# A hybrid transformer block on one core: the mixer's TensorE order written out, and work moved between its blocks

## The chip, the cores and the metric

The kernel runs on one core of a Trainium2 chip. A core has five engines with a queue of instructions each: TensorE (PE in the profile; its weight loads are shown apart as PEld) multiplies matrices, VectorE (DVE) and ScalarE (ACT) work on elements, GpSimd (POOL) works on elements in SBUF too, and SyncE (SP) issues the transfers (DMA) between the chip's memory and the core's SBUF. TensorE writes its results to PSUM, from where VectorE or ScalarE take them. Each queue is worked through in its order; an instruction that has to wait for another engine holds up all that stand behind it in the same queue.

The metric is the device time of one execution in microseconds (us). The median of three executions of the kernel before is 1883.2 us (1882.77 to 1884.28).

## The reference

Input x has 4 sequences of 256 tokens with 512 channels, in float32. Four residual parts follow each other, each behind a layer norm: attention, a feed-forward with a row and column selection, the mixer, and the same feed-forward again. All that matters here happens in the mixer, a state-space layer with 128 heads of 64 channels in 8 groups:

```
proj = input_states @ in_proj_w.T            # gate 8192, x 8192, B 8*128, C 8*128, dt 128
xBC  = silu(causal_conv4(proj[x, B, C]) + conv_b)
dA   = softplus(dt + dt_bias) * -exp(A_log)
y    = state space recurrence(x, B, C, dA, dt) + D * x      # group g: 16 heads share B[g], C[g]
g    = y * silu(gate)
g    = group rms norm(g) * norm_w                            # over each group's 1024 channels
out  = g @ out_w.T
```

The recurrence is a masked product over earlier tokens: for a head, y[i] is the sum over j <= i of (C[i] . B[j]) * exp(cum[i] - cum[j]) * dt[j] * x[j], with cum the running sum of dA. The output is x plus the mixer's out, through the last feed-forward.

## The kernel before

The mixer (`mixer`, from line 784) keeps the normed input in SBUF, split into a high and a low part (`mx0`, `mx1`), since every large product is made as three products of high and low parts (`mm3`, lines 113 to 115; so a row L113, L114 or L115 may belong to any of them). The tiles tell which: `pp` is a projection, `pog` an out product.

The 8192 channels are worked through in 64 blocks of 128 channels (two heads); eight blocks make a group. For block i:

- `projected("x", i)`: 24 matmuls of 512 columns into `pp`, a PSUM tile of two banks with two buffers. `conv` (lines 959 to 974) reads it: one ScalarE pass, three VectorE taps (L969), one ScalarE SiLU (L973).
- `product` (L1043): the weighted values of block i - 1, 32 matmul instructions from factors `em` and the turned values `xd` into `pyy`. `gated` (lines 1050 to 1067) adds D * x, multiplies by the gate, writes the result to memory (`spill`) and adds its square to the group's sum `sq` on GpSimd.
- `projected("g", i)`: 24 matmuls, then SiLU to `gt` on ScalarE.
- `differences` (lines 996 to 1014): the factors exp(cum[i] - cum[j]) of the two heads, from a row `r` of cumulated sums that a DMA spreads over the partitions (`rows`); VectorE, GpSimd and 18 ScalarE instructions. `weighted` (L1017) multiplies them by the group's masked scores `gm`.
- `turned` (lines 1019 to 1035): eight transposes of x into two one-bank tiles `trx` of the pool `m_m` (tag "m", two buffers), each evacuated by VectorE to `xd` with dt as a factor.

A group's scores (`scores`, lines 976 to 989) come from B and C, which are projected and convolved like x; `pg` lies in the same "m" buffers. A group's out product cannot start before its norm is known, so it runs one group late: in blocks 1 to 7 of the next group, `recall` reads eight spilled tiles of gated values back (`gr`), splits them into `gh`, and `partial` makes 24 matmuls into `pog`, also in "m"; `scaled` (L1114) adds the result to x. The weights of the out product come per block: `out_weights` (lines 1072 to 1082) loads 256 KB into `wor` (two buffers), scales on ScalarE (L1078) and takes the low part on VectorE (L1079) into `wo` (eight buffers, one per block of a group).

The input weights stream through `wr` (three buffers); `prepare` splits each piece of 128 columns two projections ahead, the high part on ScalarE (L105), the low part on GpSimd for the first five pieces and on VectorE afterwards (L106).

What sets the order: the source records the operations in the loop of lines 1150 to 1202, and a planner then orders each engine's queue by its own estimate of the times. So TensorE's order in the mixer is the planner's. It puts, for example, six matmuls of the next block's x ahead of block i's transposes, and sets an out product between the two halves of the transposes. In the attention part the order of TensorE is written by hand already (`tc.manual_schedule`). Each engine's queue, SP's too, is fixed when the program is built.

Of the kernel before, what the change touches and what calls it, by code (L numbers as in the profile page):

```python
# [9 lines left out]
F32 = mybir.dt.float32  # L10
# [21 lines left out]
NCL = 64  # L32
FH = (NCL + C) // 2
EPS = 1e-5


COLS = {}
# [40 lines left out]
def hybrid_kernel(  # L78
# [705 lines left out]
    def mixer(feed, later):  # L784
        with ExitStack() as es, ExitStack() as inner:
# [189 lines left out]

            def scores(bt, ct):

                gm = p2.tile([P, B, 3, P], F32, name="gm", tag="gm")
                for b in range(B):
                    pg = ps.tile([P, 3, P], F32, name="pg", tag="m")  # L980
                    k0, k1 = bt[:, b * L : b * L + P], bt[:, b * L + P : (b + 1) * L]
                    q1 = ct[:, b * L + P : (b + 1) * L]
                    nc.tensor.matmul(
                        pg[:, 0:2, :].rearrange("p s i -> p (s i)"), k0, ct[:, b * L : (b + 1) * L],
                        start=True, stop=True,
                    )
                    nc.tensor.matmul(pg[:, 2, :], k1, q1, start=True, stop=True)
                    nc.vector.tensor_tensor(gm[:, b], pg, tri.rearrange("p (s i) -> p s i", s=3), ALU.mult)
                return gm

            def rows(h):
                r = p2.tile([P, NT], F32, name="r", tag="r", bufs=2)
# [26 lines left out]
            def turned(n, x2):  # L1019

                xd = p2.tile([P, TT, P], F32, name="xd", tag="xd", bufs=1)
                for half in range(2):
                    yield xd
                    hs = slice(half * 4, half * 4 + 4)
                    tr = ps.tile([P, 4, P], F32, name="trx", tag="m")
                    for q in range(4):
                        c = half * 4 + q
                        nc.tensor.transpose(tr[:, q, :], x2[:, c * P : (c + 1) * P], ident)  # L1028
# [6 lines left out]
                yield  # L1035

            def product(xd, es2):
                py = ps_y.tile([P, B, L], F32, name="pyy", tag="pyy")
# [80 lines left out]
            order = [("b", 0), ("c", 0)]  # L1119
            for n in range(NB):  # L1120
                order += [("x", n), ("g", n)]
                if n % GB == 6 and n // GB + 1 < G:
                    order.append(("b", n // GB + 1))
                if n % GB == 7 and n // GB + 1 < G:
                    order.append(("c", n // GB + 1))
            at = {v: i for i, v in enumerate(order)}

            def projected(kind, n):
# [12 lines left out]
                return pp  # L1141

            bt = conv(projected("b", 0), NB, "gb", 3)
            ct = conv(projected("c", 0), NB + G, "gb", 3)
            gms = {0: scores(bt, ct)}
# [4 lines left out]
            for i in range(NB + 1):  # L1150
                g, gi = divmod(i, GB)
                if i < NB:
                    x2 = conv(projected("x", i), i, "x2", 2)
                if 1 <= i <= NB:
                    m = i - 1
                    px2, gt, xd, em = stage.pop(m)
                    py = product(xd, em)
                    sq = sqs.get(m // GB)
                    sqs[m // GB] = gated(m, px2, gt, py, sq)
                if i < NB:  # L1160
                    pp = projected("g", i)
# [8 lines left out]
                if gi == 0 and i >= GB:  # L1170
                    todo = [(g - 1, t) for t in range(TT)]
                if gi == 1 and i >= GB:
                    rgs[g - 1] = root(sqs.pop(g - 1))
                if i < NB:
                    turning = turned(i, x2)
                    xd = next(turning)
                    next(turning)
                for _ in range(PER.get(gi, 0)):
                    if recalled:
                        q, t, hl = recalled.pop(0)  # L1180
                        po = ps.tile([P, C], F32, name="pog", tag="m")
                        for half in range(2):
                            partial(po, q, hl[half], half)
                        scaled(q, t, po)
                if i < NB:
                    for _ in turning:
                        pass
                    if gi == 6 and g + 1 < G:
                        bt = conv(projected("b", g + 1), NB + g + 1, "gb", 3)
                    if gi == 7 and g + 1 < G:  # L1190
                        ct = conv(projected("c", g + 1), NB + G + g + 1, "gb", 3)
                        gms[g + 1] = scores(bt, ct)
                    for e in em:
                        weighted(e, gms[g])
                    stage[i] = (x2, gt, xd, em)
                for _ in range(PER.get(gi + 1, 0) if i < NB else 0):
                    if todo:
                        q, t = todo.pop(0)
                        recalled.append((q, t, [recall(q, t, half) for half in range(2)]))
                if gi >= 6 and g < G:  # L1200
                    ks = {6: (0, 1, 2, 3), 7: (4, 5, 6, 7)}[gi]
                    wos.setdefault(g, []).extend(out_weights(g, k) for k in ks)

            es_p.close()
            ps_o = pool("m_o", 4, space=PSUM, **freed)
# [52 lines left out]
def arrange(inputs):  # L1258
# [12 lines left out]
    for n in range(NB):  # L1271
        order += [NB + n, n]
        g, gi = divmod(n, GB)
        if g + 1 < G and gi == 6:
            order.append(2 * NB + g + 1)
        if g + 1 < G and gi == 7:
            order.append(2 * NB + G + g + 1)
# [49 lines left out]
```

## Time and profile before

| what | us |
|---|---|
| median of three executions | 1883.2 |
| the profiled execution | 1881.0 |
| its span, first to last instruction | 1879.2 |
| TensorE busy in the span | 1812.6 |
| VectorE busy | 1464.7 |
| ScalarE busy | 1367.7 |
| GpSimd busy | 397.0 |

The mean TensorE clock granted in the span is 0.989 of the full one. The mixer's blocks run from about 410 to 1795 us. The last feed-forward ends the program.

How to read the lines that follow. A line of a group or of the timeline names source line, engine, operation, output tile <- input tiles and shape. In the timeline the first two numbers are the start and the length in us, and a bracket gives how long the engine was idle before and what ended that. In the list of waits the three numbers are us in total, how often, and the longest. An engine's instructions overlap a little, so a stream's pace is read from start to start. Two facts about this kernel's lines: a matmul's end is modelled, and weighted values and scores show twice as many matmul instructions as the source has calls.

Over the mixer the starts of successive products (`pyy`) give the time of a block. One group, blocks 32 to 40:

| from product to product | us |
|---|---|
| blocks 32 to 33 | 28.4 |
| 33 to 37, each | 20.3 |
| 37 to 38, 38 to 39, 39 to 40 | 25.7, 27.0, 18.3 |
| eight blocks | 180.6 |

### The profile page before, as it was taken

The page shows a single profiled execution, that of the slowest core. Times are in us where ns is not written, and L with a number is a line of the kernel's source. Part 1 is how long each engine was busy: PE and PEld are TensorE (multiplying, and loading weights), DVE is VectorE, ACT ScalarE, POOL GpSimd, SP SyncE. Part 2 cuts the span into 40 slices and gives each one's busy share as a digit, 9 for nine tenths or more (in the row PEclk, how much of TensorE's full clock was granted, in tenths as well). Part 3 has the DMA queues.
Part 4 walks back from the last instruction along what each step waited for, and adds up shares of the span by engine and source line. Part 5 has one row for each costly group of instructions (what it writes and reads, how often), then busy time and mean ns, then how long its engine had stood idle before and what let it go on. Part 6 is the DMA issues. An engine that isn't in the chain of part 4 may idle for free.

```text
span 1879.2 us, 29896 instructions
## 1 busy us (share of the span) xinstructions
PE 1812.6 (96%) x10706; PEld 1450.4 (77%) x10706; DVE 1464.7 (78%) x2317; ACT 1367.7 (73%) x2809; POOL 397.0 (21%) x380
## 2 busy tenths in 40 slices
PE   7999988899999999999999999999999999999997
PEld 6777767677778787887787787878887888787787
DVE  5566667789997779778977787778778877877777
ACT  6666675378897778777876786778777876877754
POOL 6332230012321111221221121112221211121200
PEclk9999999899999999999999999999999999999999
DMA  4000000135555545544545455544444545455341
GB/s 144 1 1 1 22 15 13 37 99 170 185 182 166 156 148 173 152 157 146 185 140 172 144 173 155 165 147 162 157 157 140 179 145 164 152 159 161 113 125 50
DMA packets 152772, 240.35 MB, mean 128 GB/s; under 512 B 12464, under 2 KB 77616, under 8 KB 152624
## 3 DMA queue, kind: packets, MB, share of 16 engines
q1 hardware_dynamic: 152624, 238.44, 39.8%
q8 instruction: 84, 1.38, 0.3%
q14 instruction: 64, 0.52, 0.1%
HBM read 202.75 MB, written 35.65 MB: 127 GB/s over the span
## 4 chain that ended last, share of the span: by engine, by line
PE 79%; DVE 9%; ACT 7%; issue 2%; DMA 2%; POOL 1%; SPq 0%; DVEq 0%; ACTq 0%; POOLq 0%
PE pp L113 12%; PE pp L114 12%; PE pp L115 12%; PE pyy L1043 9%; PE pog L113 6%; PE pog L115 6%; PE pog L114 6%; PE trx L1028 3%; ACT e L475 2%; DVE acc L969 2%; PE ptr L491 1%; DMA wor<-in_wout_dram 1%; PE pq L113 1%; PE pq L114 1%; PE pq L115 1%
## 5 line engine op out<-in xcount | busy, mean ns | idle before, releaser
L113 PE MATMUL pp<-mx,w 128*128 128x512 f32 (+1 forms) x1160 | 465.2, 401 | 7.9 <-DVE acc L969 7.4
L114 PE MATMUL pp<-mx,w 128*128 128x512 f32 (+1 forms) x1160 | 454.0, 391 | 0.0
L115 PE MATMUL pp<-mx,w 128*128 128x512 f32 (+1 forms) x1160 | 453.7, 391 | 0.0
L969 DVE SCALAR_TENSOR_TENSOR acc<-pp,cw_s,acc 128x1012 f32<-128x1012 f32 (+2 forms) x240 | 305.3, 1272 | 23.0 <-ACT acc L962 22.3
L1017 DVE TENSOR_TENSOR em<-em,gm 128x1536 f32<-128x1536 f32 x128 | 228.6, 1786 | 94.3 <-ACT em L1011 85.9
L113 PEld LDWEIGHTS pp<-mx,w 128*128 128x128 f32 x1160 | 218.4, 188 | 65.7 <-issue 10.2
L1005 POOL TENSOR_SCALAR_AFFINE_SELECT r<-r 128x512 f32<-128x512 f32 x128 | 148.6, 1161 | 521.9 <-DMA r<-cumd 394.8
L1066 POOL TENSOR_TENSOR sq<-sq,acc 128x1024 f32<-128x1024 f32 x55 | 132.6, 2410 | 582.1 <-ACT acc L1065 582.1
L115 PEld LDWEIGHTS pp<-mx,w 128*128 128x128 f32 x1160 | 218.4, 188 | 45.5 <-issue 0.4
L114 PEld LDWEIGHTS pp<-mx,w 128*128 128x128 f32 x1160 | 218.6, 188 | 40.6 <-issue 0.7
L105 ACT CAST w<-wr 128x512 fp32r<-128x512 f32 x144 | 88.5, 615 | 188.9 <-PE pp L114 150.2
L113 PE MATMUL pog<-wo,gh 128*128 128x512 f32 x512 | 204.7, 400 | 0.0
L115 PE MATMUL pog<-wo,gh 128*128 128x512 f32 x512 | 200.0, 391 | 0.0
L1010 ACT ACTIVATE em<-r,col_t 128x128 f32<-128x128 f32 x512 | 165.0, 391 | 48.1 <-PE pyy L1043 46.5
L114 PE MATMUL pog<-wo,gh 128*128 128x512 f32 x512 | 200.0, 391 | 0.0
L1043 PE MATMUL pyy<-em,xd 128*64 128x256 f32 (+1 forms) x2048 | 189.1, 329 | 2.4 <-DVE em L1017 2.4
L1043 PEld LDWEIGHTS pyy<-em,xd 128*64 128x64 f32 x2048 | 133.9, 137 | 63.8 <-issue 21.8
L1013 ACT ACTIVATE em<-r,col_t 128x128 f32<-128x128 f32 x512 | 166.5, 388 | 0.0
L1001 DVE TENSOR_SCALAR em<-r,col_t 128x128 f32<-128x128 f32 x512 | 137.9, 332 | 12.1 <-PE pyy L1043 10.1
L1029 DVE TENSOR_TENSOR xd<-trx,dt_t 128x512 f32<-128x512 f32 x128 | 86.3, 684 | 54.1 <-PE trx L1028 53.9
L106 DVE TENSOR_TENSOR w<-wr,w 128x512 fp32r<-128x512 f32 x139 | 97.6, 703 | 35.9 <-ACT w L105 35.4
L475 ACT ACTIVATE e<-sc,nmx 128x256 f32<-128x256 f32 (+1 forms) x256 | 104.0, 441 | 21.0 <-DVE nmx L469 20.9
(290 smaller groups left out, 3187.2 us busy)
## 6 DMA issues: line engine op xcount, KB each, us to landing
wr<-in_win_dram SPq DMA_DIRECT2D x287, 256.0 KB, 2.8
r<-cumd SPq DMA_DIRECT2D x128, 512.0 KB, 4.1
spill<-gb SPq DMA_DIRECT2D x63, 512.0 KB, 2.8
gr<-spill SPq DMA_DIRECT2D x120, 256.0 KB, 3.5
wor<-in_wout_dram SPq DMA_DIRECT2D x64, 256.0 KB, 3.1
out_dram<-x SPq DMA_DIRECT2D x8, 256.0 KB, 2.3
x<-in_x_dram SPq DMA_DIRECT2D x1, 1536.0 KB, 8.7
gr<-spill SPq DMA_DIRECT2D x8, 192.0 KB, 2.5
```

The lines of the kernel that those rows point to most:

```text
L113: nc.tensor.matmul(o, lh, rh, start=(first and k == 0), stop=False)
L114: nc.tensor.matmul(o, lh, rl, start=False, stop=False)
L115: nc.tensor.matmul(o, ll, rh, start=False, stop=(last and k == n - 1))
L475: nc.scalar.activation(es_[c][:, 2 * j + pr, :], sc[:, j, :], AF.Exp, bias=nm[:, j : j + 1], accum_out=rs[:, c, h : h + 1],)
L969: nc.vector.scalar_tensor_tensor(av[:, :, d:], pv[:, :, : L - d], cw_s[:, ch, tap : tap + 1], av[:, :, d:], ALU.mult, ALU.add,)
L1001: nc.vector.tensor_scalar(e[:, b, 2, :], rv[:, b, 1, :], col_t[:, h, b, 1:2], 0.0, ALU.subtract, ALU.min,)
L1005: nc.gpsimd.affine_select(rv[:, :, 0, :], rv[:, :, 0, :], pattern=[[0, B], [1, P]], compare_op=ALU.is_ge, fill=-1e30, base=0, channel_mult ...
L1010: nc.scalar.activation(e[:, b, 1, :], rv[:, b, 1, :], AF.Exp, bias=col_t[:, h, b, 2:3])
L1013: nc.scalar.activation(e[:, b, 0, :], rv[:, b, 0, :], AF.Exp, bias=col_t[:, h, b, 0:1])
L1017: nc.vector.tensor_tensor(e, e, gm, ALU.mult)
L1043: nc.tensor.matmul(py[d, b, k * P :], xd[:, 2 * b + k, d], es2[hh][:, b, 2 * k : 2 if k == 0 else 3, :].rearrange("p s i -> p (s i)"), sta ...
L1066: (nc.gpsimd if n < NB - 1 else nc.vector).tensor_tensor(sq, sq, x2, ALU.add)
```

## The change

TensorE's order in the mixer's loop is written by hand, and the loop is rearranged:

1. B and C of the next group are projected behind blocks 5 and 6 of a group instead of 6 and 7 (`NEXT`; the order of the weight blocks in memory follows).
2. Within a block, the out product of the group before comes right behind x's projection; then the weighted values of block i - 1; then the second out product where there are two; then g's projection. In block 0 of a group, where there is no out product, the weighted values come between the halves of g's projection (`between`).
3. All eight transposes stand together, behind g's projection; both "m" buffers are taken at once.
4. The scores of a group are made in its block 0: two batches before g's projection, two after it. Before, they were made at the end of block 7. `gm` has one buffer instead of two, `em` four instead of three.
5. The out weights of pieces 0 to 3 of a group are asked for in its block 7, pieces 4 to 7 in block 0 of the next group. Before, this was blocks 6 and 7.
6. The low part of the input weights is taken on GpSimd for the first 18 pieces instead of 5.
7. The last block's weighted values, and pieces 4 to 7 of the last group's out weights, stand behind the loop.

```diff
+NEXT = {5: "b", 6: "c"}
...
-                    split(pieces[i], raws.pop(i), nc.gpsimd if i < 5 else nc.vector)
+                    split(pieces[i], raws.pop(i), nc.gpsimd if i < 18 else nc.vector)
...
-                gm = p2.tile([P, B, 3, P], F32, name="gm", tag="gm")
+                gm = p2.tile([P, B, 3, P], F32, name="gm", tag="gm", bufs=1)
+                yield gm
...
-                e = p2.tile([P, B, 3, P], F32, name="em", tag="em", bufs=3)
+                e = p2.tile([P, B, 3, P], F32, name="em", tag="em", bufs=4)
...
+                trs = [ps.tile([P, 4, P], F32, name="trx", tag="m") for _ in range(2)]
+                for c in range(TT):
+                    nc.tensor.transpose(trs[c // 4][:, c % 4, :], x2[:, c * P : (c + 1) * P], ident)
+                for half, tr in enumerate(trs):
...
+            with tc.manual_schedule(engines={nc.tensor.engine}):
+                for i in range(NB):
+                    g, gi = divmod(i, GB)
                     x2 = conv(projected("x", i), i, "x2", 2)
+                    if gi == 1 and g:
+                        rgs[g - 1] = root(sqs.pop(g - 1))
+                    outers = len(recalled)
+                    if outers:
+                        outer()
+                        inner_products(i - 1)
+                    while recalled:
+                        outer()
...
+                    if gi == 0 and g:
+                        scoring = scores(group["b"], group["c"])
+                        gm = next(scoring)
+                        next(scoring)
+                        next(scoring)
+                        todo = [(g - 1, t) for t in range(TT)]
+                    pp = projected("g", i, between)
...
+                    for _ in scoring:
                         pass
+                    xd = turned(i, x2)
+                    if gi in NEXT and g + 1 < G:
+                        convolved(NEXT[gi], g + 1)
                     for e in em:
+                        weighted(e, gm)
                     stage[i] = (x2, gt, xd, em)
+                    for _ in range(PER.get(gi + 1, 0)):
+                        if todo:
+                            q, t = todo.pop(0)
+                            recalled.append((q, t, [recall(q, t, half) for half in range(2)]))
+                    ks = {7: (0, 1, 2, 3), 0: (4, 5, 6, 7)}.get(gi, ())
+                    for k in ks:
+                        q = g if gi else g - 1
+                        if q >= 0:
+                            wos.setdefault(q, []).append(out_weights(q, k))
+            inner_products(NB - 1)
+            wos[G - 1].extend(out_weights(G - 1, k) for k in range(4, 8))
```

`outer()` is one tile's out product with its scaling; `inner_products(m)` is `product` and `gated` of block m; `convolved` is the projection and convolution of B or C.

More of the change, by code (lines that the diff above doesn't have):

```diff
@@ L988, in scores @@
                     nc.vector.tensor_tensor(gm[:, b], pg, tri.rearrange("p (s i) -> p s i", s=3), ALU.mult)
-                return gm
+                    yield
             def rows(h):
@@ L1021, in turned @@
                 xd = p2.tile([P, TT, P], F32, name="xd", tag="xd", bufs=1)
-                for half in range(2):
-                    yield xd
+                trs = [ps.tile([P, 4, P], F32, name="trx", tag="m") for _ in range(2)]
+                for c in range(TT):
+                    nc.tensor.transpose(trs[c // 4][:, c % 4, :], x2[:, c * P : (c + 1) * P], ident)
+                for half, tr in enumerate(trs):
                     hs = slice(half * 4, half * 4 + 4)
[L1025 to L1028, printed above, removed]
                     nc.vector.tensor_tensor(
@@ L1034, in turned @@
                     )
-                yield
+                return xd
             def product(xd, es2):
@@ L1121, in mixer, with projected @@
                 order += [("x", n), ("g", n)]
[L1122 to L1125, printed above, removed]
+                if n % GB in NEXT and n // GB + 1 < G:
+                    order.append((NEXT[n % GB], n // GB + 1))
             at = {v: i for i, v in enumerate(order)}
-            def projected(kind, n):
+            def projected(kind, n, between=lambda: None):
                 i = at[kind, n]
@@ L1140, in projected, with convolved, outer, inner_products @@
                     project(w, pp, slice(half * 512, half * 512 + 512))
-                return pp
-            bt = conv(projected("b", 0), NB, "gb", 3)
-            ct = conv(projected("c", 0), NB + G, "gb", 3)
-            gms = {0: scores(bt, ct)}
+                    if half == 0:
+                        between()
+                return pp
+            group = {}
+            def convolved(kind, g):
+                at_ = NB if kind == "b" else NB + G
+                group[kind] = conv(projected(kind, g), at_ + g, "gb", 3)
+            def outer():
+                q, t, hl = recalled.pop(0)
+                po = ps.tile([P, C], F32, name="pog", tag="m")
+                for half in range(2):
+                    partial(po, q, hl[half], half)
+                scaled(q, t, po)
+            def inner_products(m):
+                px2, gt, xd, em = stage.pop(m)
+                py = product(xd, em)
+                sqs[m // GB] = gated(m, px2, gt, py, sqs.get(m // GB))
+            convolved("b", 0)
+            convolved("c", 0)
+            scoring = scores(group["b"], group["c"])
+            gm = next(scoring)
+            for _ in scoring:
+                pass
             rr = {h: rows(h) for h in range(2)}
@@ L1149, in mixer, with between @@
             PER = {1: 2, 2: 1, 3: 1, 4: 1, 5: 1, 6: 1, 7: 1}
-            for i in range(NB + 1):
-                g, gi = divmod(i, GB)
-                if i < NB:
+            with tc.manual_schedule(engines={nc.tensor.engine}):
+                for i in range(NB):
+                    g, gi = divmod(i, GB)
                     x2 = conv(projected("x", i), i, "x2", 2)
[L1154 to L1161, printed above, removed]
+                    if gi == 1 and g:
[6 more added lines that the diff above has]
+                        outer()
+                    def between():
+                        if i and not outers:
+                            inner_products(i - 1)
+                    if gi == 0 and g:
+                        scoring = scores(group["b"], group["c"])
+                        gm = next(scoring)
+                        next(scoring)
+                        next(scoring)
+                        todo = [(g - 1, t) for t in range(TT)]
+                    pp = projected("g", i, between)
                     gt = p2.tile([P, NT], F32, name="gt", tag="gt", bufs=1)
@@ L1169, in mixer @@
                             rr[h + 2] = rows(h + 2)
[L1170 to L1184, printed above, removed]
@@ L1185, in mixer @@
-                if i < NB:
-                    for _ in turning:
-                        pass
[L1188 to L1192, printed above, removed]
+                    for _ in scoring:
+                        pass
+                    xd = turned(i, x2)
@@ L1193, in mixer @@
+                    if gi in NEXT and g + 1 < G:
+                        convolved(NEXT[gi], g + 1)
                     for e in em:
-                        weighted(e, gms[g])
+                        weighted(e, gm)
                     stage[i] = (x2, gt, xd, em)
[L1196 to L1199, printed above, removed]
@@ L1200, in mixer @@
-                if gi >= 6 and g < G:
-                    ks = {6: (0, 1, 2, 3), 7: (4, 5, 6, 7)}[gi]
-                    wos.setdefault(g, []).extend(out_weights(g, k) for k in ks)
+                    for _ in range(PER.get(gi + 1, 0)):
[7 more added lines that the diff above has]
+                            wos.setdefault(q, []).append(out_weights(q, k))
@@ L1273, in arrange @@
         g, gi = divmod(n, GB)
[L1274 to L1277, printed above, removed]
+        if g + 1 < G and gi in NEXT:
+            order.append(2 * NB + (0 if NEXT[gi] == "b" else G) + g + 1)
     blocks = wi[: (2 * NB + 2 * G) * P].reshape(-1, P, KC, P)[order]
```

## The prediction

> **What bounds the kernel now.** I read the page's shares and slices first, then the TensorE waits, then the timeline of one change of group. In the first view the reader is to see that TensorE alone is near full, and that from slice 9 on (the mixer, 410 to 1795 us) it shows nine tenths or more at a granted clock of one.
>
> ```profile
> PE 1812.6 (96%) x10706; PEld 1450.4 (77%) x10706; DVE 1464.7 (78%) x2317; ACT 1367.7 (73%) x2809; POOL 397.0 (21%) x380
> ...
> PE   7999988899999999999999999999999999999997
> ...
> PEclk9999999899999999999999999999999999999999
> ```
>
> Busy time hides small holes, so I go by starts. In the timeline matmuls of 512 columns start 0.227 us apart:
>
> ```profile
> 1246.59 0.47 PE L113 MATMUL pp<-mx,w 128*128 128x512 f32 x1 [0.88 <-DVE acc L969]
> 1246.90 0.39 PE L114 MATMUL pp<-mx,w 128*128 128x512 f32 x1
> 1247.13 0.40 PE L115 MATMUL pp<-mx,w 128*128 128x512 f32 x1
> 1247.36 0.40 PE L113 MATMUL pp<-mx,w 128*128 128x512 f32 x1
> ```
>
> A block of the steady part has 72 of them (24 for x, 24 for g, 24 for one out product): 16.3 us. Its product of weighted values takes 2.75, its eight transposes 0.79, and each change between kinds about 0.1. That makes 20.2; products start 20.3 us apart in blocks 2 to 5 of a group (1130.3, 1150.6, 1170.9). So there TensorE has no hole worth having. All that can be gained lies at the change of group: from product to product eight blocks later 180.6 us pass (1101.9 to 1282.5), while the work is 6 x 20.2 + 2 x 5.45 (B, C) + 17.4 (first block: no out product, eight score matmuls) + 27.5 (second block: two out products, group sum) = 177.1. Hence 3.5 us per change, seven changes, 24 us: the whole prize. The waits name its larger part:
>
> ```profile
> PE pp L113 <- DVE acc L969: 7.4, 8, 1.1
> ...
> PE pg L983 <- ACT acc L973: 2.8, 4, 0.9
> ```
>
> What now costs nothing, and why: a group's eight out-weight pieces pass through two "wor" buffers. A piece is a DMA, a ScalarE scaling, a VectorE remainder, and the next DMA starts when that remainder ends:
>
> ```profile
> 1259.87 0.37 SPq L1075 DMA_DIRECT2D wor<-in_wout_dram  x1
> 1262.86 0.33 SPq L1075 DMA_DIRECT2D wor<-in_wout_dram  x1
> 1265.31 0.33 SPq L1075 DMA_DIRECT2D wor<-in_wout_dram  x1
> ```
>
> ```profile
> 1262.08 0.75 DVE L1079 SCALAR_TENSOR_TENSOR wo<-wor,nw_s,wo 128x512 fp32r<-128x512 f32 x1 [0.41 <-ACT wo L1078]
> ...
> 1263.77 0.72 ACT L1078 ACTIVATE wo<-wor,nw_s 128x512 fp32r<-128x512 f32 x1 [1.72 <-DMA wor<-in_wout_dram]
> ...
> 1264.53 0.75 DVE L1079 SCALAR_TENSOR_TENSOR wo<-wor,nw_s,wo 128x512 fp32r<-128x512 f32 x1 [0.51 <-ACT wo L1078]
> ...
> 1272.84 0.74 DVE L1079 SCALAR_TENSOR_TENSOR wo<-wor,nw_s,wo 128x512 fp32r<-128x512 f32 x1
> ```
>
> The reader sees one buffer turn: DMA at 1259.87, ScalarE at 1263.77, VectorE to 1265.28, next DMA at 1265.31: 5.4 us. The last piece is done at 1273.6; the first out product that uses them ends at 1303.2, so some 24 us of cover.
>
> **The change, part by part.**
>
> *B and C behind blocks 5 and 6, scores split 2 + 2 around g.* Same 48 projection matmuls, same 16 score instructions. An out product and a weighted product now stand between a conv and the next use of its PSUM buffer, 13.8 us, against conv's 1.2 + 3 x 1.19 and its queue: the L969 wait goes. C's conv is a block early: the L983 wait goes.
>
> *Out products first.* The weighted product gets 5.45 us more time; its factors are weighted a block ahead, before g. Gain: the 2.4 us of such waits, mostly in group 0. Price: an out product follows x, so its recalled halves and weights are wanted 5.45 us into the block instead of after g, product and transposes, 9.5 us earlier. For the halves the reads have a block of 20.2 us: nothing. For the weights see below.
>
> *Transposes in eights.* 0.79 + 0.12 instead of 2 x (0.35 + 0.12): 0.03 us a block, 2 us in all. They need both "m" banks, so they wait for the evacuation of what lay there.
>
> *Splits on GpSimd up to piece 17.* 13 more remainders move from VectorE (0.60 us start to start) to GpSimd (1.63 us in its L106 row): 7.8 us off VectorE in group 0; there are two blocks of slack for each, beside 2.4 us sums and 0.8 us selects.
>
> *Four factor buffers, one mask buffer.* The mask's last reader is block 7's weighting, a block before. Nothing.
>
> *TensorE in written order.* Before, x's matmuls filled the waits. In the first block after the scores the chain of transposes, masks and x's SiLU is now bare: some 14 of 24 x matmuls that ran beside it move behind it, +3 us once. In group 0 ScalarE changes table four times a block instead of 2.8: 4 x 1.29 + 10.8 of work = 15.9 against 15.5 per block: +2 us. In the steady part that sum with the recalls is 17.0 under 20.2: covered. At the end the last product has no out product between its transposes, and the last group's weights come later: +3.
>
> *Out weights 4 to 7 moved from block 7 to the next group's block 0.* This decides. In the built program's order, with t from the start of block 0's x: TensorE x 5.45, scores 6.7, half g 9.4, product 12.35, half g 15.1, scores 16.3. VectorE can't touch the gated value before 12.35; then stand in its queue gb 1.19, its gate 1.13, seven differences at 0.25 (0.21 in a row, 0.33 alone) and among the last of them masks 2 and 3 at 0.47: 17.3. The transposes wait for both: TensorE loses 0.6, and x of block 1 ends at 23.25, the group sum at 24.95, the first half of the first out product at 27.7. Behind the masks VectorE has two xd 0.6, two weightings 1.67, a w remainder and a gh remainder 0.6: 23.2. SP's queue is in order: a weight load that waits for that w remainder, then a recall that waits for that gh remainder, and only behind them the DMAs of pieces 4 and 5, at 23.7 and 24.1. With 3.1 us to landing: 26.8 and 27.2. ScalarE's next entry there is the fourth recalled half (buffer free at 27.4), then piece 4: VectorE done 29.45; piece 5 behind a table load and an exp: 31.95. Pieces 6 and 7 take the buffers of 4 and 5 one turn (5.4 us) later: 35.1 and 37.4. TensorE waits in place, in four gaps, and ends the second half at 38.1 instead of 30.4: 7.7. Queued behind it are the weighted product, the second out product and g of block 1, so nothing covers it. Bounds: if the DMAs of 4 and 5 were not held up on SP, pieces 6 and 7 are ready some 4 us earlier (stall 4); with landing at that row's longest, 5.3 instead of 3.1, twice in the chain, 12. I take 7.7, which the turn of the trace gives.
>
> [...]
>
> [...]
>
> **Sum.** Against the profiled execution, 1881.0 us for a span of 1879.2: per change 177.1 + 0.6 + 7.7 = 185.4 against 180.6: +4.8, times seven +34; +3 start, +2 group 0, +3 end: 1923. The shown median is 2.2 above the profiled execution, but the other runs spread by 1.5: I say 1924.
>
> **Rivals.**
> 1. *The weights are there* (faster). If SP issues pieces 4 to 7 early enough, only 0.6 of the 8.3 stays: 177.7, -2.9 x 7 = -20, +8 for the rest: 1869. For: block 0 is short on TensorE, and VectorE's and ScalarE's queues are planned. Against: two buffers at 5.4 us a turn, and the order above. It decides where the stall at the weights falls below 1.7 us a change (3.5 - 0.6 - 8/7).
> 2. *Half the stall*, SP not held up: 4 + 0.6: 181.7, +1.1 x 7 = +8, +8: 1897.
> [...]
> 4. *ScalarE becomes the bound*: four table changes and waits in its queue make 21.5 out of 17.0 in the blocks where TensorE needs 20.2: +1.3 x 35 = +45 more, 1968. Against: it is 73% busy.
>
> **How the numbers follow.** Main case 0.58 (own range 1908 to 1940), weights there 0.10, half 0.12, longer 0.13, ScalarE 0.07. The range leaves out the first rival and the top tenth: 1888 to 1957. A measurement of this kernel can tell 0.2%, 3.8 us, from no change. Faster 0.10; same 0.02, from the low edge of the second; slower 0.88.
>
> **What would show it.** Right: TensorE waits at the first out product of each group, released by wo's VectorE remainder and by ScalarE's wo, about 7 x 7 us; no wait of pp on acc nor of pg on acc; a wait of trx on gm of about 0.6; products still 20.2 apart in blocks 2 to 5; PEclk unchanged. Wrong: no TensorE wait on wo, a clock below one at the changes, or 21 us and more between products of the steady blocks.

## The result, and the profile after

The changed kernel takes 1969.2 us (median of four runs, 1967.1 to 1973.9) against 1883.7 of the kernel before beside it: 1.0457 times as long, 95% interval 1.0437 to 1.0477. The prediction said 1924, 1888 to 1957: it had the direction right and the size too small.

The profiled execution has a span of 1967.1 us, 87.9 more than before. The first part of its page and two rows of its slices, after, answer to the rows shown of before:

```profile
PE 1853.4 (94%) x10706; PEld 1470.0 (75%) x10706; DVE 1486.2 (76%) x2304; ACT 1479.7 (75%) x2888; POOL 381.5 (19%) x393
...
PE   8999988898989998999899989998999899989997
...
PEclk9999999899998999999899989998999899989999
```

The number of matmul instructions is the same, 10706, yet TensorE is busy 40.8 us longer. From slice 10 on eight slices of the busy share show an 8, the last six of them four slices apart, which is about a group of blocks. In the granted clock an 8 stands at six of the seven changes of group. Before, both rows were 9 throughout the mixer. The TensorE waits of after name what TensorE stands for (us in total, how often, the longest):

```profile
PE pog L115 <- ACT wo L1079: 34.1, 28, 3.0
PE trx L1027 <- ACT acc L975: 9.3, 6, 2.9
PE trx L1027 <- DVE gm L991: 6.8, 7, 1.4
...
PE pp L115 <- DVE acc L971: 2.2, 2, 1.9
PE pyy L1044 <- DVE em L1020: 2.1, 1, 2.1
...
PE pog L116 <- DVE wo L1080: 2.0, 7, 0.3
```

28 waits on the out weights are four in each of the seven changes of group. The wait of `pg` on `acc` is gone, that of `pp` on `acc` fell from 8 to 2. One change in the timeline of after (compare the buffer turn of before):

```profile
1153.75 0.97 SPq L1076 DMA_DIRECT2D wor<-in_wout_dram  x2
...
1158.79 0.75 DVE L1080 SCALAR_TENSOR_TENSOR wo<-wor,nw_s,wo 128x512 fp32r<-128x512 f32 x1 [0.65 <-ACT wo L1079]
...
1158.81 0.50 PE L115 MATMUL pog<-wo,gh 128*128 128x512 f32 x1 [2.42 <-ACT wo L1079]
1159.57 0.33 SPq L1076 DMA_DIRECT2D wor<-in_wout_dram  x1
...
1161.34 0.75 DVE L1080 SCALAR_TENSOR_TENSOR wo<-wor,nw_s,wo 128x512 fp32r<-128x512 f32 x1 [0.50 <-ACT wo L1079]
1161.36 0.80 PE L115 MATMUL pog<-wo,gh 128*128 128x512 f32 x1 [0.57 <-ACT wo L1079]
1162.12 0.33 SPq L1076 DMA_DIRECT2D wor<-in_wout_dram  x1
...
1164.63 0.80 PE L115 MATMUL pog<-wo,gh 128*128 128x512 f32 x1 [1.26 <-ACT wo L1079]
...
1166.93 0.75 DVE L1080 SCALAR_TENSOR_TENSOR wo<-wor,nw_s,wo 128x512 fp32r<-128x512 f32 x1 [1.57 <-ACT wo L1079]
1166.95 0.79 PE L115 MATMUL pog<-wo,gh 128*128 128x512 f32 x1 [0.32 <-ACT wo L1079]
...
1168.89 4.97 PE L1044 MATMUL pyy<-em,xd 128*64 128x256 f32 x32
```

All four late pieces hold TensorE. The DMAs of pieces 6 and 7 leave when the remainders of pieces 4 and 5 end (1159.54 and 1162.09), as foretold. The matmuls between are shown with 0.80 us instead of 0.40, and the weighted values behind them take 4.9 us from start to start instead of 2.75. The same stretch by windows (behind the engines of a row stand the granted clock, the DMA share and GB/s):

```profile
core 0: us, PE busy (x) PEld busy (x) DVE busy (x) ACT busy (x) POOL busy (x), PEclk, DMA share, GB/s
1137.00:1153.00 16.00, 15.14 (x99) 12.30 (x98) 15.81 (x21) 13.11 (x19) 4.07 (x3) 1.00 0.43 139
1153.00:1169.00 16.00, 11.14 (x31) 5.64 (x32) 10.48 (x14) 13.53 (x22) 0.00 (x0) 0.71 0.62 190
1169.00:1174.00 5.00, 5.00 (x33) 3.42 (x34) 2.83 (x4) 1.95 (x7) 1.66 (x1) 0.57 0.52 184
1174.00:1190.00 16.00, 16.00 (x75) 13.31 (x75) 12.23 (x19) 10.98 (x24) 3.35 (x3) 1.00 0.50 164
```

The granted clock, 1.00 ahead of the waits, is halved in their midst (1159.7 to 1173.3 in the clock's record) and comes back only 4.4 us after the out product has ended (1168.9). All seven changes show such a stretch, 10.2 to 13.7 us long, and group 0 shows five of 3.4 us. In the mixer of before there is none.

By the starts of the products, the 87.9 us lie here:

| part of the span | before | after | more | said |
|---|---|---|---|---|
| to the first product | 421.6 | 427.9 | +6.3 | +3 |
| group 0, product 0 to 7 | 121.5 | 139.9 | +18.4 | +2 |
| seven groups, product 7 to 63 | 1246.0 | 1307.6 | +61.6 | +34 |
| from there to the end | 90.1 | 91.7 | +1.6 | +3 |

Of the seven, the first six go from 180.4 to 189.7 each (said: 180.6 to 185.4).

### The profile page after: what moved, and what is told of

The parts are those of the page before. It is cut to its first block, busy times and chain, and to the rows that moved or that the text cites. A ratio compares the mean times of both kernels' runs of the same rounds, so it can differ in the third digit from the quotient of the medians.

```text
span 1967.1 us, 29911 instructions
## 1 busy us (share of the span) xinstructions
PE 1853.4 (94%) x10706; PEld 1470.0 (75%) x10706; DVE 1486.2 (76%) x2304; ACT 1479.7 (75%) x2888; POOL 381.5 (19%) x393
## 3 DMA queue, kind: packets, MB, share of 16 engines
q1 hardware_dynamic: 152624, 238.44, 37.4%
## 4 chain that ended last, share of the span: by engine, by line
PE 70%; ACT 12%; DVE 7%; DMA 6%; issue 3%; POOL 1%; SPq 0%; DVEq 0%; ACTq 0%; POOLq 0%
PE pp L115 11%; PE pp L116 11%; PE pp L117 11%; PE pyy L1044 8%; PE pog L115 5%; PE pog L116 5%; PE pog L117 5%; PE trx L1027 3%; DMA wor<-in_wout_dram 3%; ACT e L477 2%; DMA wr<-in_win_dram 1%; PE ptr L493 1%; ACT em L1016 1%; ACT em L1013 1%; PE pq L115 1%
## 5 line engine op out<-in xcount | busy, mean ns | idle before, releaser
L1020 DVE TENSOR_TENSOR em<-em,gm 128x1536 f32<-128x1536 f32 x128 | 252.4, 1977 | 72.7 <-ACT em L1016 72.7
L1008 POOL TENSOR_SCALAR_AFFINE_SELECT r<-r 128x512 f32<-128x512 f32 x128 | 106.6, 833 | 801.2 <-DMA r<-cumd 578.4
L115 PE MATMUL pog<-wo,gh 128*128 128x512 f32 x512 | 210.8, 412 | 34.9 <-ACT wo L1079 34.1
L1067 POOL TENSOR_TENSOR sq<-sq,acc 128x1024 f32<-128x1024 f32 x55 | 138.5, 2519 | 384.0 <-ACT acc L1066 384.0
L116 PE MATMUL pog<-wo,gh 128*128 128x512 f32 x512 | 209.6, 409 | 2.0 <-DVE wo L1080 2.0
L117 PE MATMUL pog<-wo,gh 128*128 128x512 f32 x512 | 205.6, 402 | 0.0
L1044 PE MATMUL pyy<-em,xd 128*64 128x256 f32 (+1 forms) x2048 | 194.5, 345 | 2.5 <-DVE em L1020 2.1
L1013 ACT ACTIVATE em<-r,col_t 128x128 f32<-128x128 f32 x512 | 172.7, 390 | 20.2 <-PE pyy L1044 18.4
L1016 ACT ACTIVATE em<-r,col_t 128x128 f32<-128x128 f32 x512 | 168.1, 389 | 0.4
L1004 DVE TENSOR_SCALAR em<-r,col_t 128x128 f32<-128x128 f32 x512 | 142.8, 334 | 16.9 <-PE pyy L1044 12.0
L115 PEld LDWEIGHTS pog<-wo,gh 128*128 128x128 f32 x512 | 98.2, 192 | 72.0 <-ACT wo L1079 51.2
L108 DVE TENSOR_TENSOR w<-wr,w 128x512 fp32r<-128x512 f32 x126 | 87.9, 697 | 78.9 <-ACT w L107 77.8
L107 ACT CAST gh<-gr 128x512 fp32r<-128x512 f32 (+1 forms) x128 | 77.4, 609 | 79.9 <-PE pog L116 60.0
```

Of the source, the lines that this page charges most:

```text
L107: nc.scalar.copy(hl[0], v)
L115: nc.tensor.matmul(o, lh, rh, start=(first and k == 0), stop=False)
L116: nc.tensor.matmul(o, lh, rl, start=False, stop=False)
L117: nc.tensor.matmul(o, ll, rh, start=False, stop=(last and k == n - 1))
L1004: nc.vector.tensor_scalar(e[:, b, 2, :], rv[:, b, 1, :], col_t[:, h, b, 1:2], 0.0, ALU.subtract, ALU.min,)
L1008: nc.gpsimd.affine_select(rv[:, :, 0, :], rv[:, :, 0, :], pattern=[[0, B], [1, P]], compare_op=ALU.is_ge, fill=-1e30, base=0, channel_mult ...
```

## The experiments

All ratios are to the kernel before, beside it on the same chip. The theory after this profile: late weights stall the first out product of each group, and the waits then halve the clock. The rival: it is the written order as a whole, which bares whatever wait comes next.

**Out weights early.** Undoes part 5 alone.

```diff
-ks = {7: (0, 1, 2, 3), 0: (4, 5, 6, 7)}.get(gi, ())
+ks = {6: (0, 1, 2, 3), 7: (4, 5, 6, 7)}.get(gi, ())
```

> The kernel after with one part undone: out weights 0 to 3 of a group asked for in its block 6, 4 to 7 in block 7, as before. Theory (late weights stall the first out product of each group, and the waits then halve TensorE's clock): in the kernel after, the last weight of a change at 1167.7 comes 9.2 us after the time at which an unhindered stream would have used it (12 matmuls at 0.227 from 1156.0), and the half clock behind it costs 2.9 more; both go in all seven changes, -85 us at most, 1885 to 1900, no TensorE wait on wo, granted clock 1.0 from block 8 on. Rival (TensorE's written order as a whole is what costs; without this wait the next one is bared): -20 or less, 1945 or more, with new waits of trx, pp or pyy of 5 us and more per change.

1924.8 us, 1.0218 (1.0192 to 1.0245): half of what the theory promised at most (85). No wait on `wo` is left, but another has grown from 6.8 us to 34.7 (waits of this kernel):

```profile
PE trx L1027 <- DVE gm L991: 34.7, 15, 4.2
PE trx L1027 <- ACT acc L975: 10.7, 7, 2.9
```

A change takes 184.1 us. With the weights in time, the transposes of a group's first block wait 5.0 us for masks 2 and 3, which stand in VectorE's queue behind the differences (ends at 1127.5 and 1130.0 in the change that I followed). Some 1.8 us of that are one of these differences, which took 2.09 us instead of its usual 0.28 and ended just behind a sum of GpSimd's that had begun before it. The timelines of this kernel:

```profile
1127.11 2.35 POOL L1067 TENSOR_TENSOR sq<-sq,acc 128x1024 f32<-128x1024 f32 x1 [0.72 <-ACT acc L1066]
1127.45 2.09 DVE L1004 TENSOR_SCALAR em<-r,col_t 128x128 f32<-128x128 f32 x1
1129.46 0.54 DVE L991 TENSOR_TENSOR gm<-pg,tri 128x384 f32<-128x384 f32 x1
```

All seven changes of this kernel have such a difference, of 1.9 to 2.1 us. The half clock is still there, 3.4 to 6.8 us long at every change. So the late weights explain 44 us of 85, and the rest lay under them.

**Fillers in the waits.** Leaves all waits and gives TensorE something to do.

```diff
 for k in range(4):
+    filled((6, 4, 6, 2)[k])      # matmuls into the next product's tile, which nobody reads
     nc.tensor.matmul(po, gh, wh, start=False, stop=False)
+    filled(2)
     nc.tensor.matmul(po, gh, wl, start=False, stop=False)
```

> The kernel after, with 26 matmuls that nobody reads put into the waits of each group's first out product (ahead of pieces 4 to 7: 6, 4, 6 and 2; and two between the high and the low part of each piece), written into the next product's PSUM tile before that product starts it afresh. The waits on the weights stay as they are. Theory (the waits halve the clock): clock stays 1.0 at the seven changes, the product behind the waits takes 2.75 us instead of 4.91, and about 2.9 us per change come back: -20, about 1949. Rival (the clock falls for another reason, or costs nothing since TensorE waits anyway): 1969 or, by fillers that come too late, up to +5.

1954.8 us, 1.0383 (1.0361 to 1.0406): 14.4 us less than after, with 26 matmuls more in every change. Windows of this kernel, over waits and product:

```profile
core 0: us, PE busy (x) PEld busy (x) DVE busy (x) ACT busy (x) POOL busy (x), PEclk, DMA share, GB/s
...
1153.00:1165.00 12.00, 9.75 (x38) 6.17 (x36) 6.14 (x9) 10.20 (x16) 0.00 (x0) 1.00 0.61 189
1165.00:1169.00 4.00, 4.00 (x37) 2.78 (x37) 3.64 (x3) 3.22 (x11) 0.00 (x0) 1.00 0.48 146
```

The clock stays at 1.00 at all seven changes, though the weights are as late as before. A change takes 187.7 us instead of 189.7. So the half clock comes from TensorE's idle time and is a cost of its own: 2 us per change, some 0.9 less than expected.

**Transposes of group 0 later.** They move behind the next block's x, as an answer to the 9.3 us of waits for x's SiLU.

```diff
+if 1 <= i <= GB:
+    px2, gt, _, em = stage[i - 1]
+    stage[i - 1] = (px2, gt, turned(i - 1, px2), em)
...
-xd = turned(i, x2)
+xd = turned(i, x2) if i >= GB else None
```

> The kernel after, with the transposes of blocks 0 to 7 alone moved behind the next block's x projection (one projection, 5.45 us, later). Theory (in group 0 the written order bares the wait of the transposes for x's SiLU, and each such wait brings a window of half clock): the 9.3 us of trx waits on acc go, and with them four to five windows of half clock at 1.7 us: -15, about 1954. Rival (in group 0 ScalarE is the bound, 15.9 us of work in blocks of 15 to 16 us): the wait moves to another place, pyy on em or pp on w: within 4 us of 1969.

1968.8 us, 1.0457 (1.0432 to 1.0482): nothing. The rival was right in that the wait moves; group 0 even takes 145.8 us instead of 139.9, which eats up a start shorter by 4.5. This kernel's waits:

```profile
PE pg L986 <- DVE xd L1030: 5.6, 2, 3.4
PE pp L115 <- DVE acc L971: 5.0, 2, 3.5
PE pyy L1044 <- DVE em L1020: 4.3, 4, 2.1
PE pyy L1044 <- DVE xd L1030: 3.9, 4, 3.1
```

**Both edits.**

> Both edits together: out weights in blocks 6 and 7, and transposes of group 0 behind the next x projection. If both causes are separate and additive: about 1893 - 15 = 1878, which is below the kernel before (1883.7). If group 0 is bound by ScalarE: about 1893.

1923.9 us, 1.0217 (1.0195 to 1.0239), as with early weights alone. Each wait that I took out of the written order had laid the next one bare. So the next runs took the order itself.

**The planner's order, all places of the work as changed.** The written order's block is dropped; weights stay late, scores stay in block 0, the out product stays ahead in the source.

```diff
-with tc.manual_schedule(engines={nc.tensor.engine}):
+with ExitStack():
     for i in range(NB):
```

> The kernel after, with TensorE's order in the mixer's loop left to the planner; all places of the work (B and C, scores, out weights) stay as changed. Theory (late weights stall a fixed order, another order can put other matmuls into the wait): most of the 9.2 + 2.9 us per change and of group 0's 18 us come back: 1900 to 1920. Rival (it is the place of the weights and scores, not the order): within 10 us of 1969.

1875.7 us, 0.9959 (0.9944 to 0.9974): faster than before, by more than the theory allowed. Of the waits on `wo` one of 0.2 us is left; the longest list entry in the mixer and the windows around a change:

```profile
PE trx L1027 <- DVE gm L991: 7.8, 8, 2.1
```

```profile
1085.80:1104.60 18.80, 18.49 (x116) 15.11 (x115) 17.86 (x25) 15.90 (x24) 3.80 (x3) 1.00 0.49 155
1104.60:1120.60 16.00, 16.00 (x91) 12.71 (x91) 12.62 (x15) 15.23 (x26) 0.00 (x0) 1.00 0.73 236
```

TensorE is busy all of the 16 us in which it stood before. The weights are hardly earlier: their DMAs leave at 1104.8 to 1111.6, the last remainder ends at 1117.1, 9.7 us after the first half of the first out product (11.5 in the kernel after; over the seven changes 9.6 to 12.0 against 11.0 to 12.1). But TensorE does the weighted values at 1107.6, out product work that is ready, and matmuls of g from 1115.9 on, ahead of what is late. A change takes 178.9 us. The difference in TensorE's order is small: in groups 2 to 7 the two traces differ in 14 of a group's matmuls. The twelve of the late half stand behind the weighted values, among the second out product and g, and one of x's stands ahead of each half of the first block's transposes. VectorE's and ScalarE's queues, which the planner lays out around TensorE's, differ in more places, so this run does not change TensorE's order alone.

**The planner's order in group 0 alone.**

```diff
-with tc.manual_schedule(engines={nc.tensor.engine}):
-    for i in range(NB):
+for i in range(NB):
+    with tc.manual_schedule(engines={nc.tensor.engine}) if i >= GB else ExitStack():
```

> The kernel after, with TensorE's order left to the planner in blocks 0 to 7 alone, by hand from block 8 on. Theory (in group 0 the fixed order bares waits that x's matmuls filled before; the shifted transposes only moved them): start and group 0 go back to about the time of before, product of block 7 at 545 instead of 568, -20: about 1949. Rival (ScalarE is the bound in group 0, with four table loads per block): products still 20 us apart there, within 5 us of 1969.

1941.1 us, 1.0304 (1.0287 to 1.0321). Product 0 to 7 takes 124.9 us instead of 139.9; the later changes are shorter too, 188.7 instead of 189.7, and the start stays at 427.7. The order by hand is written for each block by itself here: at the first block of each later group some of the next x's matmuls still stand ahead of the transposes. Group 0 by windows, in turn of before, after and this kernel:

```profile
421.00:543.00 122.00, 118.21 (x660) 92.36 (x658) 115.66 (x152) 110.00 (x209) 34.89 (x22) 1.00 0.54 179
```

```profile
428.00:568.00 140.00, 126.33 (x674) 98.71 (x676) 119.79 (x147) 123.05 (x214) 43.44 (x32) 0.94 0.48 151
```

```profile
427.00:553.00 126.00, 121.12 (x680) 94.12 (x680) 115.80 (x139) 120.88 (x212) 48.69 (x33) 1.00 0.50 163
```

ScalarE (the fourth number behind the comma) has 120.9 us of work in 126: it is nearly the bound there, from 110.0 before. Group 0 under the planner is 3.4 us longer than before, which I put down to ScalarE; no run tests that by itself. The other 15 us are the order. The rows divide them: in the kernel after TensorE stands still for 13.7 us (140.00 - 126.33), in this one for 4.9, and it works 5.2 us longer on nearly the same matmuls, at 0.94 of the clock.

**Scores back in block 7,** with early weights, to remove the mask wait under the written order. To make room, `em` has three buffers again.

```diff
-gm = p2.tile([P, B, 3, P], F32, name="gm", tag="gm", bufs=1)
+gm = p2.tile([P, B, 3, P], F32, name="gm", tag="gm", bufs=2)
...
+if gi == 7 and g + 1 < G:
+    scoring = scores(group["b"], group["c"])
+    following = next(scoring)
```

> The kernel with out weights early (1924.8), and in addition the four score batches at the end of block 7 instead of in the next group's block 0, with two mask buffers again (and three factor buffers, for room). Theory (with the weights there, the next wait of the change is that of the transposes for masks 2 and 3, 5.0 us at each, and its half clock, 6.8 us long): both go, 184.3 - 5 - 1.5 = 178 per change, -40: about 1885. Rival (the masks are late because VectorE is behind as such, and then something else waits): within 10 us of 1925.

1926.7 us, 1.0235 (1.0199 to 1.0272): a miss. Its four runs spread from 1919.6 to 1936.6, and the profile is of the shortest. Of the wait on `gm` 1.0 us is left; in its place (waits of this kernel):

```profile
PE trx L1027 <- ACT acc L975: 35.3, 13, 4.3
```

**The same with the planner in group 0.**

> The same, with group 0 left to the planner too. If the causes add up: 1885 - 20 = 1865, below the kernel before. If group 0 is bound by ScalarE: 1885.

1897.4 us, 1.0079 (1.0064 to 1.0094): 29 less than without, more than the 20 expected; but it does not reach the kernel before, since its base was too low by 40. Most of the 29 are not group 0's. By the traces product 0 to 7 goes from 139.3 to 134.5 us, and the seven groups behind it from 1260.2 to 1244.2. There too the blocks are written each by itself, and at every first block six or more of the next x's matmuls, twelve in group 1, stand ahead of the transposes. The wait on `acc` fell from 35.3 us to 1.7. So most of the gain goes with a few matmuls in front of an operand that is late. The other queues moved as well, so these matmuls are not shown to be all of it.

**Late weights alone, in the kernel before.**

```diff
-ks = {6: (0, 1, 2, 3), 7: (4, 5, 6, 7)}[gi]
+ks = {7: (0, 1, 2, 3), 0: (4, 5, 6, 7)}.get(gi, ())
```

> The kernel before with part 5 alone: out weights 4 to 7 of a group asked for in the next group's block 0, all else as it was, TensorE's order by the planner. Theory now (lateness costs only under an order that can't step round it): 1878 to 1890. Rival (late weights cost by themselves): 9 us and more at each of seven changes, 1945 or more.

1882.8 us, 1.0006 (0.9993 to 1.0019): no difference. But the weights are not late in this kernel, so it does not test the theory. The out product stands behind g here, as before, and in six of seven changes the last remainder is done 4.6 to 5.1 us ahead of the end of the first half (in the first just in time; in the kernel before about 27 us ahead, in the first 30). Part 5 alone only uses up cover. The 44 us come of it together with part 2, which moves the out product ahead, and with an order that keeps TensorE in place. That late weights can be stepped round is shown by the planner's order above, where they are late and TensorE waits for them 0.2 us.

**Cover by hand.** Only block 1 of a group is written anew.

```diff
-outer()
-inner_products(i - 1)
+partial(pos2[0], pending[0][0], pending[0][2][0], 0)
+inner_products(i - 1)
+partial(pos2[1], pending[1][0], pending[1][2][0], 0)
+for po, (q, t, hl) in zip(pos2, pending):
+    partial(po, q, hl[1], 1)
+    scaled(q, t, po)
```

> The kernel after, still with a written order, with one change in block 1 of a group: first half of the first out product, weighted values, first half of the second out product, and only then the second halves of both. Theory (what was queued behind the waits is the cover that was missing): 5.5 us of work stand ahead of the late pieces, whose last remainder comes 10.5 us after the first half; the stall falls from 9.2 to about 2.8 and the half clock goes with it: -6.4 to -8.8 per change, 1907 to 1924. Rival (both banks of the tag are held longer, so that the transposes or the next product wait instead): 1945 or more.

1919.6 us, 1.0198 (1.0173 to 1.0223). A change takes 182.8 us, 6.9 less. The waits of this kernel show the rest of the stall, about 2.6 us per change, as worked out; a half clock of 3.4 us stays in each.

```profile
PE pog L115 <- ACT wo L1079: 15.4, 11, 2.2
...
PE pog L116 <- DVE wo L1080: 2.9, 10, 0.3
```

So the stall of 10 us is hidden as far as there is ready work in front of it.

**Planner's order, and GpSimd's share as before** (`i < 5` instead of `i < 18`).

> The kernel after with TensorE's order by the planner (1875.7), and with only the first five input-weight remainders on GpSimd, as before, instead of 18. Theory (that part has two blocks of slack): within 3 us of 1876. Rival (GpSimd's slower remainders, with the selects and sums beside them, are what makes group 0 longer than before: product of block 7 at 549.7 against 543.1): 1869 to 1871.

1872.8 us, 0.9951 (0.9935 to 0.9966): 2.9 below the run with 18. In total this part costs nothing that can be told, as the prediction had it. But that is two differences against each other: by the traces group 0 takes 131.8 us instead of 126.0 with five, and the seven groups behind it 1224.6 instead of 1230.8. The rival is refuted; why the later groups are shorter was not looked into.

**Gaps alone.** A tail behind the kernel before, with matmuls of 512 columns, 0.23 us from start to start, and made waits. It ran once.

```diff
+burst(90)
+for cols in ([], [512], [512] * 2, [512] * 3, [512] * 4, [512] * 5, [512] * 6, [512] * 8):
+    gap(cols)                     # so many VectorE copies between two matmuls
+    burst(90)
+for n, k in ((3, 3), (3, 6), (2, 3), (1, 3), (0, 3)):
+    for _ in range(4):
+        gap([512] * n)
+        burst(k)
+    burst(90)
```

> The kernel before with a tail that only measures: 90 matmuls of 512 columns on end, then TensorE waits for VectorE; single waits of eight lengths (about 0.6 to 7 us), then four waits in a row with three (or six) matmuls between, in five sizes; 90 matmuls after each. [...] Rival (what counts is how little TensorE does in a stretch of some us, not one gap): a row of four waits of 2 us halves the clock as a single one of 4 us does, and for longer.

Gaps are from the start of the last matmul ahead to the start of the next:

| gaps, us | half clock behind them, us |
|---|---|
| one of 0.71, 1.31, 2.04 | none |
| one of 2.77 | 3.4 |
| one of 3.49 | none |
| one of 4.20 | 3.4 |
| one of 4.94, one of 6.38 | 6.8 each |
| four of 0.71, three matmuls between | none |
| four of 1.31 to 1.54, three between | 6.8 |
| four of 2.03 to 2.27, three between | 10.2 |
| four of 2.76 to 3.00, three between | 17.1 |
| four of 2.76 to 3.00, six between | 3.4 and 13.7, with 3.4 at full clock between |

Windows of this kernel, around the row of 2.03 to 2.27, around that of 1.31 to 1.54, and in that of 0.71:

```profile
2178.00:2192.00 14.00, 8.32 (x19) 5.33 (x20) 5.25 (x11) 0.00 (x0) 0.00 (x0) 0.63 0.00 1
2192.00:2215.00 23.00, 21.14 (x90) 16.38 (x88) 1.65 (x4) 0.00 (x0) 0.00 (x0) 1.00 0.00 0
2215.00:2222.50 7.50, 5.71 (x13) 4.02 (x14) 1.65 (x4) 0.00 (x0) 0.00 (x0) 0.55 0.00 0
2242.00:2250.00 8.00, 6.73 (x26) 4.41 (x25) 0.90 (x4) 0.00 (x0) 0.00 (x0) 1.00 0.00 0
```

The rival holds: four gaps of 2.0 to 2.3 us halved the clock for 10.2 us, a single one of 4.2 for 3.4; and four of 1.3 to 1.5 halved it too, where a single one of 3.5 did not. The half-clock stretches of this tail begin and end on one grid of 3.41 us. So do all twelve in the mixer of the kernel after: from the start of the first change's, 589.6, to that of the fourth's, 1159.7, are 570.1 us, 167 cells. I laid the grid over the tail and counted in each cell the share of it in which a matmul ran (0.23 us each). Every cell at full clock with a share up to 0.36 is followed by a cell at half clock, and every one from 0.43 up by one at full clock. The cells at half clock fit too when their work is counted at half; counted in full they do not. So the single gap of 3.49, which fell across two cells (0.57 and 0.43 of work), did no harm, and that of 2.77, which lay within one (0.33), brought 3.4 us of half clock.

## Why the prediction was wrong in size

The forecast was +42 us, and +87.9 came. Three terms of the sum were too small by about 16 us each: group 0 (+18.4 instead of +2), the late weights' stall (10.0 instead of 7.7 us, seven times) and the clock, which was put at nothing (2.2 us, seven times). The start gave another 3. By this sum, any one of the three as forecast would have brought the time inside the range. The terms add up to some 6 us more than was missed: the change that they are read from is one of the longer ones, and the last of the seven grew by only 5.5 us.

**Bound and steady block: right.** Products in blocks 2 to 5 are 20.2 us apart, as summed. The rival in which ScalarE sets the steady block (1968) has the right time for a wrong reason: 21.5 apart did not come.

**B and C earlier, out products first, transposes in eights, GpSimd's share: right.** The two waits that made the prize are gone or nearly so. The planner's version of the change shows how much of the prize was to be had: 178.9 us per change against 180.4, where the sum said 177.1.

**Late weights: right in place and mechanism, too small by 2.3 us.** From the start of block 0's x (1127.5) the sum and the trace stand like this:

| step, us from the start of x | said | trace |
|---|---|---|
| product starts (half of g ends) | 9.4 | 9.7 |
| masks 2 and 3 done | 17.3 | 18.2 |
| first half of the out product done | 27.7 | 28.7 |
| first late DMA leaves | 23.7 | 26.3 |
| remainders of pieces 4, 5 | 29.45, 31.95 | 32.1, 34.6 |
| remainders of pieces 6, 7 | 35.1, 37.4 | 37.9, 40.2 |
| second half done | 38.1 | 41.4 |

The stall is 41.4 - 28.7 - 2.7 = 10.0 instead of 7.7. The turn of the two buffers held; the 2.6 us came in ahead of the first DMA, 0.9 of it up to the masks and 1.7 in one weighting of the factors, which took 3.44 us where the sum had 1.67. The timelines of VectorE and GpSimd, after:

```profile
1146.41 3.44 DVE L1020 TENSOR_TENSOR em<-em,gm 128x1536 f32<-128x1536 f32 x1
```

```profile
1145.83 2.40 POOL L1067 TENSOR_TENSOR sq<-sq,acc 128x1024 f32<-128x1024 f32 x1 [3.17 <-ACT acc L1066]
```

GpSimd's sum lies over it for 1.82 us, and it is 1.69 longer than the usual 1.75. In the kernel after, 24 of the 128 weightings began while a GpSimd instruction ran. Two of them, with 0.05 and 0.06 us of it left, took 1.76 and 1.75; the other 22 took 2.2 to 3.5, and these alone are longer than 1.77 us. In the 19 beside a sum the excess is what that sum still had to run, less 0.13 to 0.14 us (1.82 - 1.69 in this row). In 18 others GpSimd began second, and the weighting took its 1.75.

**Masks: 0.6 said, 1.0 measured** (6.8 us in seven waits). Under the weights' stall it looked small; with the weights early it was 5.0. The prediction did not ask what would be late next if the weights were in time, which is the case of its first rival (1869). With the weights in time the run took 1924.8, which refutes that rival. That 1924.8 is also the forecast number is chance.

**The clock: the step that failed.** I put the four gaps at 1.9, 1.8, 2.5 and 1.5, took each by itself and left the clock at one. The trace of before, where the longest TensorE wait in the mixer is 1.1 us, had not shown what gaps of that size do. From start to start, 0.23 of matmul included, they were 2.8, 1.2, 1.9 and 0.95 in the change shown, with up to 0.8 between the matmuls of a piece, and the clock halved for 13.7 us. The longest gap does not tell this: in the tail a single one of 2.77 brought 3.4 us of half clock and one of 3.49 none. The work in a cell of the 3.41 us grid does: in the tail every full-clock cell with a share up to 0.36 was followed by one at half clock, and a row of four gaps of 1.31 to 1.54 was enough for 6.8 us of it. For this change the cost is 4.9 - 2.75 = 2.2 us in the product, beside 0.7 in the last two matmuls ahead of it, which the 10.0 holds. The fillers, which took the half clock away alone, brought back 2.0. For the change shown the sum then closes: 177.1 + 10.0 + 2.2 + 1.0 = 190.3, and the trace has 190.2 (1137.2 to 1327.4).

**Group 0 and the start: the other step that failed, and the larger in relation.** I priced table loads at +2 and took the bared waits to be in the first block after the scores alone. The table loads were about right: 26 in the seven blocks instead of 16, +1.4 a block where I had said +1.2, and group 0 is 3.4 us longer than before when the planner orders it. But 15 us more are the written order in group 0: with no out product to stand in between, TensorE waits for x's SiLU (9.3 us, nearly all of it in four blocks), for a conv and for a factor. Together it stands still 8.8 us longer than under the planner and works 5.2 us longer, with five half-clock stretches where the planner's order has none. The start's +6.3 was not tested by itself; the planner in group 0 left it as it was (427.7), the planner in all of the loop brought 423.7, and later transposes 423.4.

**The range** gave 13 in 100 to a longer stall, 12 us per change, with 1.7 more for a half clock: 1965, which is the nearest to what happened; that its total comes so near is in part luck. No run shows the 1.7: the half clock cost 2.2 us in the product of the change shown, and the fillers brought back 2.0 per change. The case gave the seven groups +76 and the rest +8, and the runs +61.6 and +26.3. What the range lacked was a case in which group 0 goes wrong: without the 20 us that it and the start took beyond the forecast, the time would have been 1949, inside.

## What to carry to other kernels

A written order fixes every wait in place: before writing one, list for each instruction in it what is ready behind it, and price a late operand by the ready work that stands in front of it: weights about 10 us late cost nothing that shows in the waits under an order that stepped round them, and 44 us under one that did not. When a wait is removed from a fixed order, ask which comes next: here early weights gave half of what the theory promised at most, and the two removals tried after them gave nothing. Sum TensorE's work over stretches of a few us, not the longest gap alone, when you judge whether its clock will hold: in the tail four gaps of 1.3 to 1.5 us halved it, and a single one of 3.5 did not.

## What was not expected of the hardware

A row of four TensorE gaps of 1.3 to 1.5 us, with three matmuls between, halved the clock for 6.8 us, where a single gap of 3.5 us left it whole and one of 2.8 did not. In the kernel after, four gaps of at most 2.8 us (in the change shown) brought a half-clock stretch of 13.7 us, longer than the waits themselves, and filling them with matmuls that nobody reads brought back 14.4 us in all.

VectorE's weighting of 128x1536 took between 2.2 and 3.5 us in 22 of 128 cases in the kernel after, each time with a GpSimd instruction already at work when it began (in one case it ended 0.001 us later), and 1.74 to 1.76 in all others, also in the 18 in which GpSimd began second. So in nearly all of these 40 cases it is not the overlap that costs, but who begins first. In the kernel before none of 128 took over 2.2; six of them began 0.07 to 0.12 us behind a GpSimd select and took 1.75 all the same, while the select took 2.3 to 4.7.
